# The first layer's input turned by TensorE's transposes and ScalarE's copies, in place of VectorE's block transposition of a second load, for 17 of 64 batches

## The chip, the cores and the metric

The kernel runs on one core of a Trainium2 chip. The metric is the device time of one execution in microseconds (us), as the median of several runs.

## What is computed

The input x is 64 batches of 256 rows of 256 numbers (float32); a mask adj of 256 x 256 is common to all batches. Two layers follow each other, and each adds to x the result of a graph attention and then that of a feed-forward part:

```
x = x + gat0(layernorm(x), adj, W, a)      # 4 heads of 64, leaky slope 0.2, softmax over the mask, elu
x = x + layernorm(x) @ weight.T + bias
x = x + gat1(layernorm(x), adj, W, a)      # one head of 256, slope 0.01, relu
x = x + moe(layernorm(x))                  # 8 experts, the top 2 of each row by a router, gelu between two matmuls
```

The change concerns the very first matmul of a batch, h @ W of the first attention. TensorE contracts over partitions, so it needs x with the features on the partitions, that is, x transposed.

## The kernel before, in words

**Tiling.** A batch is held as 2 tiles of 128 rows (`NT` = 2), and its 256 features as 2 halves of 128 (`KT` = 2). The normalisation isn't applied to x: its mean is taken out of the weights (`center`), and its scale `rstd` is multiplied in behind the matmul.

**The order of the work.** The program is laid out by hand as one sequence of steps, three for each batch (`TICKS`). Each batch is a generator (`batch_layers`), and each yield hands over a rank: a positive rank ends the batch's part in this step and gives its place in the next, smaller ranks first; a negative rank only moves the rest back within the same step. A batch is in flight for some twenty steps, so that six or seven batches overlap. Work of other kinds is begun beside them: the preparation of weights (`setup`, with the packing of the experts' weights, L280 to L296) over the first batches; the routing of each chunk of 4 batches (`route`, L1067); and from the second chunk on two expert pairs per batch (`expert_pair`, L870: rows gathered by an expert, its two matmuls `hidden` and `product`, and a scatter to the output by GpSimd). Each engine then works through its own instructions strictly in that order.

**A batch, by its lines.** In its first step x0 (`xin`, loaded three batches ahead, L96) is read by VectorE for the statistics of the norm (L379, L380). Two steps later the input is turned (L606), and one step after that it is projected (`projected`, L470), on TensorE; ScalarE takes exponentials (L478) and VectorE scales (L486). The scores' terms go to DRAM and come back spread over all partitions (L616, L551); up to batch 17 ScalarE's queue issues these two DMAs, later SP's (`terms_queue`, L545, with `SETTLED` = 18). VectorE forms the scores z (L567), TensorE multiplies them with q (`attended`, L581), VectorE divides and adds (L588, L634, L643 to L646). x1 is transposed by TensorE (`transposed`, L454, copied by ScalarE, L460), multiplied with the feed-forward weights (pf, L655), and becomes x2 (L662). x2 is transposed in the same way; then follow layer 1's projection (L505), scores (L524, L529), attention (pv with tiles of 128 x 257, L581 again), `rel` (L683), x2 again (L689), the normalised rows xng (L712) and base (L718), their transposition and the router's product pl (L743), copied to lg by VectorE (L747).

**How the input is turned before.** For the first layer a second load (`load_blocks`, L101 to L110) brings x into `xblk`: four DMAs of 64 KB for each batch, in pieces of 64 numbers (256 bytes), so arranged that a transposition within blocks of 32 x 32 gives the wanted layout. They are issued by SP two batches ahead (`BLOCKS_AHEAD` = 2), at the place where a batch is turned. One VectorE instruction (`turned`, L115, L117) then writes `xT`. The three other transpositions of a batch (x1, x2, xng) are made by `transposed`: four TensorE transposes against `ident` into one bank of PSUM, and one copy by ScalarE. Given `blocks=True`, as for xng, it takes every second column of x for each half, the order of features which the weights of the first layer have too (`rows` in `gnn_weights`).

**Buffers.** The tiles `xT` come from a ring of four, the PSUM banks from a ring of eight that all matmuls and transposes share (`bank`, L79).

Of the kernel before, what the change touches and what calls it, by code (L numbers as in the profile page):

```python
# [9 lines left out]
F32 = mybir.dt.float32  # L10
# [5 lines left out]
P = 128  # L16
# [11 lines left out]
def kernel(  # L28
# [18 lines left out]
    B, N, D = x.shape  # L47
# [3 lines left out]
    KT = D // P  # L51
# [22 lines left out]
    work = ctx.enter_context(tc.tile_pool(name="work", bufs=2))  # L74
# [4 lines left out]
    def bank(name, shape):  # L79
        t = psum.tile([P, 2 * D], F32, tag="bank", name=name, bufs=8)  # L80
        n = 1
        for s in shape:
            n *= s
        t = t[:, :n]
        if len(shape) == 2:
            t = t.rearrange("p (a b) -> p a b", a=shape[0])
        elif len(shape) == 3:
            t = t.rearrange("p (a b c) -> p a b c", a=shape[0], b=shape[1])
        return t
# [11 lines left out]
    def load_blocks(b):  # L101


        t = io.tile([P, N // S, KT * S], F32, tag="xblk", name=f"xblk_{b}", bufs=3)
        for g in range(P // S):
            nc.sync.dma_start(
                out=t[g * S : (g + 1) * S],
                in_=x[b].rearrange("(c q) (g f) -> g q c f", q=S, g=P // S)[g],
            )
        return t  # L110
# [4 lines left out]
    def turned(dst, blocks):  # L115

        nc.vector.transpose(  # L117
            dst.rearrange("p k (c q) -> p k c q", q=S),
            blocks.rearrange("p c (a k) -> p k c a", k=KT),
        )  # L120
        return dst

    def by_block(ap):

        return ap.rearrange("p (a k) -> p k a", k=KT)

    AHEAD, BLOCKS_AHEAD = 3, 2
    PAIRED = CHUNKS[0] + CHUNKS[1] + 3
    SETTLED = CHUNKS[0] + CHUNKS[1] + CHUNKS[2] + CHUNKS[3] + 2
# [99 lines left out]
    xblk = {0: load_blocks(0)}  # L229
# [220 lines left out]
    def transposed(src, pool=work, tag="xT", bufs=4, blocks=False):  # L450
        pt = bank("pt", [KT, N])
        for t in range(NT):
            for k in range(KT):
                nc.tensor.transpose(  # L454
                    pt[:, k, t * P : (t + 1) * P],
                    by_block(src[:, t, :])[:, k] if blocks else src[:, t, k * P : (k + 1) * P],
                    ident,
                )
        dst = pool.tile([P, KT, N], F32, tag=tag, name="xT", bufs=bufs)
        nc.scalar.copy(dst, pt)  # L460
        return dst
# [72 lines left out]
    def send_terms(q, b):  # L534
# [7 lines left out]
        ud = ud.rearrange("c r -> (c r)").rearrange("(c p) -> c p", p=P)  # L542
        return ut, ud

    def terms_queue(b):  # L545

        return nc.scalar if b < SETTLED else nc.sync

    def spread_terms(b, ud, z):

        terms_queue(b).dma_start(  # L551
            out=z[:, NT - 1].rearrange("p t h i -> p (t h i)"),
            in_=rows_to_all(ud, S * S),
        )
# [36 lines left out]
    def batch_layers(b, c0, xng, lg):  # L591

        def first_norm():
            x0 = xin.pop(b)
            if b + AHEAD < B:
                xin[b + AHEAD] = load_batch(b + AHEAD)
            return x0, norm_stats(x0)[1]

        if b:
            x0, rstd = first_norm()  # L600
            yield 99
            yield 4
        xb = xblk.pop(b)
        if b + BLOCKS_AHEAD < B:
            xblk[b + BLOCKS_AHEAD] = load_blocks(b + BLOCKS_AHEAD)
        xT = turned(work.tile([P, KT, N], F32, tag="xT", name="xT", bufs=4), xb)  # L606
        if not b:
            x0, rstd = first_norm()
        yield 22
# [3 lines left out]
        if b:  # L613
            ut, ud = send_terms(q, b)
            yield -31
            terms_queue(b).dma_start(  # L616
                out=ud.rearrange("c (g r) -> g c r", g=G),
                in_=ut[2 : P : S // (NT * H), :],
            )
            yield -52  # L620
# [29 lines left out]
        xT = transposed(x1)  # L650
# [20 lines left out]
        xT = transposed(x2)  # L671
# [66 lines left out]
        xT = transposed(xe[:, :, :D], *dense_home(b), blocks=True)  # L738
# [15 lines left out]
    def dense_home(b):  # L754

        if b < ROUTED:
            return ()
        return (io, "xblk", 3) if b < ROUTED + 3 else (io, "xin", 6)
# [444 lines left out]
    def jobs():  # L1203
        b = done = taken = 0
        for c, nb in enumerate(CHUNKS + (1,) * DENSE):
            nt = nb * NT
            lg = keep.tile([P, nt, E], F32, tag="lg", name=f"lg_{c}", bufs=7)
            xng = []
            row0 = b * N
            done += nt  # L1210
            n = max(done - (E - 1) - taken, 0) if b < ROUTED else 0
            taken += n
            for i in range(nb):
                def job(b=b, c=c, i=i, nb=nb, nt=nt, n=n, lg=lg, xng=xng, row0=row0):
                    yield from batch_layers(b, i * NT, xng, lg)
                    if i == nb - 1:
                        if b >= ROUTED:
                            yield 65
                            yield from route_dense(b, lg)
                        else:  # L1220
                            yield from route(c, row0, nt, n, b == ROUTED - 1, xng, lg)
                yield job()
                b += 1
# [85 lines left out]
```

## Time and profile before

Three runs: 1524.20, 1528.13 and 1528.14 us, median 1528.13.

| Profiled execution | |
|---|---|
| its own time | 1528.82 us |
| span, first to last instruction | 1527.0 us |
| TensorE matmul / weight load, busy | 1431.3 us (94%) / 1266.2 us (83%) |
| VectorE | 1255.8 us (82%) |
| ScalarE | 1007.2 us (66%) |
| GpSimd | 871.9 us (57%) |
| mean granted TensorE clock | 0.974 of full speed |
| moved by DMA | 240.84 MB in 372852 packets, 264773 of them under 512 bytes |

Engines are PE (TensorE; PEld for its weight loads), DVE (VectorE), ACT (ScalarE), POOL (GpSimd) and SP (which issues DMAs); an engine's name with a q behind it is its queue of instructions. A line such as L117 is a line of the kernel before. In the lists of groups, "out<-in" gives the tiles written and read, x and a number how often. A list of waits gives the waiting engine, tile and line, then what it waited for, then the total in us, how often, and the longest. In a timeline the first two numbers are the start and the length in us, and a bracket at the end is the time the engine sat idle before, and what ended it.

### The profile page before, as it was taken

To read this page: it belongs to the slowest core of one execution; us is meant where nothing else is said; L and a number is where in the kernel's file an instruction comes from. 1 tells how busy PE (TensorE), PEld (TensorE's weight loads), DVE (VectorE), ACT (ScalarE), POOL (GpSimd) and SP (SyncE) were. 2 spreads that over 40 slices of the span, in tenths; PEclk is the share of its full clock that TensorE was granted. 3 is DMA by queue.
4 is the path that set the end of the run, shared out by engine and by line. 5 is a ranking of instruction groups with operands and counts; after the bars stand their busy time and mean duration, and the time that the engine had idled before them with its cause. 6 is when DMAs were issued, how large, how long until landed. Compare 5 with 4: busy or idle time off the path is not lost.

```text
span 1527.0 us, 29964 instructions
## 1 busy us (share of the span) xinstructions
PE 1431.3 (94%) x8066; PEld 1266.2 (83%) x8066; DVE 1255.8 (82%) x4436; ACT 1007.2 (66%) x2379; POOL 871.9 (57%) x845
## 2 busy tenths in 40 slices
PE   6899989899999999999999999998899989799992
PEld 5788778789898989999998989897788877678882
DVE  7889998889988888888889989899888878655541
ACT  1466666577777777777877777776678779643330
POOL 2212536355857676767667675756747676544444
PEclk9999999899999999999999999999999999989997
DMA  5752434567877878787778787877768676788743
GB/s 146 206 170 87 137 115 123 143 161 154 190 172 176 180 174 177 170 180 165 178 176 185 170 180 159 194 157 164 172 156 186 127 164 131 169 198 166 140 62 52
DMA packets 372852, 240.84 MB, mean 158 GB/s; under 512 B 264773, under 2 KB 334925, under 8 KB 372685
## 3 DMA queue, kind: packets, MB, share of 16 engines
q1 hardware_dynamic: 319768, 162.62, 43.4%
q0 software_dynamic: 48864, 66.33, 23.7%
q10 hardware_dynamic: 4052, 9.98, 2.0%
q8 instruction: 67, 1.10, 0.3%
q14 instruction: 101, 0.82, 0.2%
HBM read 150.46 MB, written 88.35 MB: 156 GB/s over the span
## 4 chain that ended last, share of the span: by engine, by line
PE 66%; DVE 18%; DMA 4%; issue 4%; ACT 4%; SPq 2%; POOL 1%; DVEq 0%; another core or an unknown queue 0%; POOLq 0%; ACTq 0%; PEldq 0%
PE pv L581 15%; PE ph L944 14%; PE py L959 14%; PE pf L655 5%; PE pq L470 5%; PE pq L505 5%; DVE z L567 4%; PE pt L454 4%; PE pl L743 2%; DMA xblk<-in_x_dram 1%; DMA out_dram<-y,xt 1%; DVE stats L379 1%; DVE x L644 1%; DVE x1b L646 1%; DVE x L662 1%
## 5 line engine op out<-in xcount | busy, mean ns | idle before, releaser
L980 POOL DMA_INDIRECT out_dram<-y,xt x258 | 413.5, 1603 | 198.2 <-issue 63.8
L581 PE MATMUL pv<-q,z 128*128 128x65 f32 (+1 forms) x2560 | 370.4, 301 | 0.3
L581 PEld LDWEIGHTS pv<-q,z 128*128 128x128 f32 x2560 | 336.6, 196 | 13.3 <-DVE z L567 0.8
L1050 POOL DMA_INDIRECT xs<-xng,pos x244 | 263.4, 1079 | 65.4 <-issue 60.0
L959 PE MATMUL py<-w2s,hT 128*128 (+1 forms) x1224 | 280.7, 380 | 5.6 <-ACT hT L950 5.5
L959 PEld LDWEIGHTS py<-w2s,hT 128*128 128x128 f32 x1224 | 229.1, 191 | 37.4 <-ACT hT L950 8.0
L944 PE MATMUL ph<-sT,we 128*128 128x256 f32 x1032 | 244.4, 387 | 12.9 <-DMA we<-wpack 6.5
L567 DVE SCALAR_TENSOR_TENSOR z<-z,q,mask 128x256 f32<-128x256 f32 x504 | 231.5, 482 | 11.8 <-DMA z<-terms 2.8
L944 PEld LDWEIGHTS ph<-sT,we 128*128 128x128 f32 x1032 | 198.7, 195 | 42.2 <-issue 7.2
L937 ACT ACTIVATE y<-y,w 128x256 f32<-128x256 f32 x258 | 113.0, 498 | 114.3 <-DVE y L969 111.5
L460 ACT COPY xT<-pt 128x512 f32<-128x512 f32 x192 | 112.8, 587 | 105.1 <-PE pt L454 77.3
L950 ACT ACTIVATE hT<-ph,we 128x256 f32<-128x256 f32 x306 | 123.7, 472 | 63.5 <-PE ph L944 39.3
L407 POOL TENSOR_SCALAR rstd<-mv 128x4 f32<-128x4 f32 (+1 forms) x66 | 15.6, 236 | 255.2 <-DVE mv L380 201.6
L425 ACT ACTIVATE off<-x,sums 128x256 f32<-128x256 f32 x256 | 129.4, 505 | 10.4 <-DVE x L662 2.6
L505 PE MATMUL pq<-wx,xT 128*128 128x259 f32 x512 | 127.1, 391 | 7.3 <-ACT xT L460 4.1
L969 DVE TENSOR_TENSOR y<-py,b2s 128x512 f32<-128x512 f32 x129 | 85.7, 685 | 57.9 <-PE py L959 41.6
L470 PE MATMUL pq<-wx,xT 128*128 128x268 f32 x512 | 128.2, 394 | 2.4 <-DVE xT L117 1.8
L655 PE MATMUL pf<-wfT,xT 128*128 128x256 f32 x512 | 125.7, 390 | 0.0
L683 ACT ACTIVATE rel<-pv,rinv 128x256 f32<-128x256 f32 x128 | 53.7, 468 | 99.6 <-DVE rinv L588 66.6
L505 PEld LDWEIGHTS pq<-wx,xT 128*128 128x128 f32 x512 | 95.3, 192 | 28.2 <-ACT xT L460 8.2
L470 PEld LDWEIGHTS pq<-wx,xT 128*128 128x128 f32 x512 | 98.0, 192 | 21.5 <-DVE wx L168 1.3
L655 PEld LDWEIGHTS pf<-wfT,xT 128*128 128x128 f32 x512 | 95.9, 197 | 11.1 <-issue 0.2
(172 smaller groups left out, 2378.0 us busy)
## 6 DMA issues: line engine op xcount, KB each, us to landing
we<-wpack SPq DMA_DIRECT2D x145, 288.0 KB
xr<-xs SPq DMA_DIRECT2D x516, 64.0 KB
z<-terms SPq DMA_DIRECT2D x46, 512.0 KB
xblk<-in_x_dram SPq DMA_DIRECT2D x256, 64.0 KB
xin<-in_x_dram SPq DMA_DIRECT2D x64, 256.0 KB
out_dram<-base SPq DMA_DIRECT2D x61, 256.0 KB
z<-terms ACTq DMA_DIRECT2D x17, 512.0 KB
out_dram<-y,xt POOLq DMA_INDIRECT x258
```

The costliest lines, as they stand in the source:

```text
L425: nc.scalar.activation(off, src[:, t, :], AF.Square, bias=sums[:, t : t + 1], scale=-float(D), accum_out=sq[:, at + t : at + t + 1],)
L470: nc.tensor.matmul(pq.rearrange("p h c -> p (h c)"), xT[:, k, t * P : (t + 1) * P], wx[:, k, :], start=(k == 0), stop=(k == KT - 1),)
L505: nc.tensor.matmul(pq, xT[:, k, t * P : (t + 1) * P], wx1[:, k, :], start=(k == 0), stop=(k == KT - 1),)
L567: nc.vector.scalar_tensor_tensor(z[:, j, :, h, :], terms, q[:, j, h, HD + 2 : HD + 3], masks[0][:, j, :].rearrange("p (t i) -> p t i", t=N ...
L581: nc.tensor.matmul(pv[:, h, :], z(j, h, t), q[:, j, h, : d + 1], start=(j == 0), stop=(j == NT - 1),)
L655: nc.tensor.matmul(pf[:, t, :], xT[:, k, t * P : (t + 1) * P], wfT[:, k, :], start=(k == 0), stop=(k == KT - 1),)
L937: nc.scalar.activation(y[:, t, :], y[:, t, :], AF.Copy, scale=w[:, t : t + 1])
L944: nc.tensor.matmul(ph[:, f, :], we[:, k * D + f * P : k * D + (f + 1) * P], xT[:, k, :], start=(k == 0), stop=(k == KT - 1),)
L950: nc.scalar.activation(hT[:, f, :], ph[:, f, :], AF.Gelu, bias=we[:, C_B1 + f : C_B1 + f + 1])
L959: nc.tensor.matmul(py[:, t, :], hT[:, f, t * P : (t + 1) * P], w2s[:, e, f * D : (f + 1) * D].rearrange("p e c -> p (e c)"), start=(f == 0 ...
L980: d = nc.gpsimd.indirect_dma_start(out=out_rows, out_offset=bass.IndirectOffsetOnAxis(ap=xt[:, t, 0:1].bitcast(I32), axis=0), in_=y[:, t, ...
L1050: d = nc.gpsimd.indirect_dma_start(out=xs_d[: E * CAP * PAIR, :], out_offset=bass.IndirectOffsetOnAxis(ap=at, axis=0), in_=xe, in_offset=None,
```

## The change

For batches 2 to 18 (`by_tensor`) the second load and the VectorE transposition fall away. In their place `transposed` takes x0, the tile that is loaded for the statistics anyway: four TensorE transposes into a bank and one ScalarE copy. In the step in which the input is turned, the rank goes from 4 to 38, behind the transposes of x2 (rank 36) and ahead of layer 1's attention (rank 40) of other batches. Batches 0 and 1 and those from 19 on are as before; the blocks of batch 19 are loaded in batch 17.

```diff
+    def by_tensor(b):
+
+        return BLOCKS_AHEAD <= b <= SETTLED
+
...
         if b:
             x0, rstd = first_norm()
             yield 99
-            yield 4
-        xb = xblk.pop(b)
-        if b + BLOCKS_AHEAD < B:
+            yield 38 if by_tensor(b) else 4
+        if b + BLOCKS_AHEAD < B and not by_tensor(b + BLOCKS_AHEAD):
             xblk[b + BLOCKS_AHEAD] = load_blocks(b + BLOCKS_AHEAD)
-        xT = turned(work.tile([P, KT, N], F32, tag="xT", name="xT", bufs=4), xb)
+        if by_tensor(b):
+            xT = transposed(x0, blocks=True)
+        else:
+            xT = turned(work.tile([P, KT, N], F32, tag="xT", name="xT", bufs=4), xblk.pop(b))
         if not b:
             x0, rstd = first_norm()
```

## Prediction

> **What bounds the kernel now.** I began with the page's totals: TensorE is busy for 94% of the span, VectorE for 82%. That is a mean over stages, and the change touches batches 2 to 18 only. So I took the starts of the block transpositions of L117 as marks: batch 2 at 27.60 us, 6 at 84.33, 9 at 126.92, 19 at 287.72, 21 at 327.54. Busy times between such marks:
>
> ```profile
> 84.33:126.92 42.59, 42.30 (x268) 38.45 (x268) 38.11 (x129) 31.12 (x84) 9.14 (x15) 0.96 0.46 139
> 126.92:287.72 160.80, 149.37 (x902) 129.85 (x901) 149.63 (x549) 101.88 (x276) 67.35 (x86) 0.97 0.40 118
> 220.11:237.82 17.71, 16.07 (x81) 13.94 (x79) 14.83 (x56) 9.19 (x27) 8.57 (x10) 0.81 0.54 153
> 327.54:427.99 100.45, 100.45 (x597) 90.54 (x596) 90.52 (x311) 76.76 (x182) 68.33 (x65) 1.00 0.80 175
> ```
> After the stretch and its length come PE, PE's weight loads, VectorE, ScalarE and GpSimd, then TensorE's granted clock. From 327 us on TensorE is never idle. From 84 to 127 it is nearly so, and a batch there takes 13.22 us. Between 127 and 288 us, ten batches of 16.1 us, both are at 93%, and the waits decide. All of VectorE's waits in that stretch, and the largest of TensorE's between 130 and 300 us:
>
> ```profile
> DVE x L662 <- issue: 2.2, 1, 2.2
> DVE q L486 <- ACT q L478: 0.9, 1, 0.9
> DVE y L969 <- DVE mv L380: 0.6, 1, 0.6
> ```
> ```profile
> PE pd L524 <- ACT ex L512: 6.3, 12, 2.0
> PE pt L454 <- DVE x L662: 4.8, 7, 1.1
> ```
> VectorE waits 3.7 us in 160.8. The rest that isn't busy lies between instructions that follow each other without a wait. TensorE waits every batch, for what hangs on VectorE. So **VectorE sets the pace from 127 to 288 us**, TensorE from 84 to 127 and after about 300. The chain of waits agrees: between 150 and 250 us it is led by VectorE lines, from 309 us on it holds TensorE alone.
>
> Last, the operations concerned:
>
> ```profile
> L117 DVE STREAM_TRANSPOSE xT<-xblk x64: 651/703/727, 9.9 to 1203.5; 128x512 f32<-128x512 f32 x64
> L454 PE MATMUL pt<-ident,xng x256: 272/283/417, 80.1 to 1330.7; 128*128 128x128 f32 x128
> L460 ACT COPY xT<-pt x31: 562/567/620, 128.3 to 286.8; 128x512 f32<-128x512 f32 x31
> ```
>
> **What the skill says.** "Vector Engine: DVE Perf Modes", The three transpose paths: VectorE turns 32x32 blocks only, into SBUF; TensorE turns a full 128x128, into PSUM. Hence the blocked second load before, and a copy after. "TensorE: Matmul & The Clock Gate", Part 4: about 275 ns for a transpose in a kernel; it doesn't count as busy for the clock. The trace has 273 ns (x) and 283 ns (xng), but pipelined. The same page, Part 1: after an idle window of about 3.4 us the clock is halved. The trace agrees: 0.81 granted over 220 to 238 us, with matmuls at half speed. "DMA: Bandwidth & Descriptors", Issuing engines are not separate DMA queues: all DMAs share the same 16 engines. This case shows contention at 68 us, below.
>
> **The change, part by part.** In the built program's order VectorE loses 17 block transpositions. TensorE gains 17 times four transposes, between those of x2 and the matmuls pv of layer 1. ScalarE gains 17 copies, each right behind the copy of x2. SP loses 68 loads.
>
> (1) *VectorE, batches 9 to 18.* At 220.11 a transposition starts, and the next instruction (L643) at 220.74: the place is worth 0.63 us, less than the 0.70 of its duration. Ten batches paced by VectorE: **-6.3 us**. Late next is TensorE: its 13.22 a batch becomes 13.72, under the 15.3 that VectorE then needs (16.1 less 0.63 and its share of waits). The loop through both holds too: from L662 to the reciprocal of layer 1 VectorE has 4.6 us of work, then 4.0; TensorE's way over x2's transposes, the new ones and pv takes 2.7, then 3.2.
>
> (2) *TensorE, batches 6 to 8.* Four blocked transposes of xng hold the engine from 110.36 to 110.87, 0.50 us; four of x take 0.44. x0 is read in blocks, as xng is: 0.50. Alone, with latency, it would be 0.68; 0.44 to 0.68 bounds it. Three batches: **+1.5 us**. In batches 9 to 18 it lies inside TensorE's waits; without this cover it would cost 5 us.
>
> (3) *ScalarE.* 17 copies of 0.57 us. Behind the copy are `rel` (L683) and the exponentials of layer 1. `rel` waits for the reciprocal, 28.9 us in 9 batches of the stretch: covered. In batches 7 and 8 it waits 1.5 us after a copy (101.95 to 103.48): covered. Uncovered: up to 0.57 each. Zero.
>
> (4) *Batches 2 to 5.* The transpositions at 27.60 and 56.84 are on the chain, with 0.62 and 0.57: **-1.2 us**. Batch 3's isn't; its z waits for a DMA: 0. At batch 5 VectorE waits for the spread terms, which left together with four block loads:
>
> ```profile
> 68.30 1.81 SPq L106 DMA_DIRECT2D xblk<-in_x_dram  x4
> 68.36 0.34 ACTq L551 DMA_DIRECT2D z<-terms  x1
> ...
> 74.24 3.75 DVE L567 SCALAR_TENSOR_TENSOR z<-z,q,mask 128x256 f32<-128x256 f32 x8 [1.64 <-DMA z<-terms]
> ```
> Here 5.86 us from issue to use; at 41.61, with no block loads beside it, 4.76. I take **-1.1 us**. Ends: 0 (the weight loads fill the room) and -1.6, the whole idle time. The 68 issues of 0.45 us that SP is rid of only bring the loads behind them forward. They are 4.5 of 240.8 MB.
>
> (5) *New waits.* The transposes wait for x0, which VectorE's statistics read two steps earlier, and for a bank. One more bank per batch moves the ring of eight on: the second half of the projection (L470) now waits for the copy of lg (L747), where before the transposes of x1 did (0.7 us in two cases). Behind it queue x1's transposes, pd and pv. At 207.9 TensorE would come to it, 208.4 with (2); lg was copied at 208.63, and is now 0.63 earlier, 208.0: no wait. Bounds 0 to 0.4 for each of ten batches; 0.
>
> (6) *Clock.* Cold stretches follow gaps without matmuls:
>
> ```profile
> 223.95 0.60 PE L454 MATMUL pt<-ident,x 128*128 128x128 f32 x4
> 225.99 0.32 PE L524 MATMUL pd<-ident,ex 128*128 128x128 f32 x1 [1.44 <-ACT ex L512]
> 226.51 0.32 PE L524 MATMUL pd<-ident,ex 128*128 128x128 f32 x1 [0.20 <-ACT ex L512]
> 226.67 4.90 PE L581 MATMUL pv<-q,z 128*128 128x65 f32 x32
> ```
> From 223.95 to 226.67 there are only transposes and waits. Then pv takes 4.90 instead of 3.68, and VectorE's 2.2 us for pf at 236 is the price. VectorE 0.63 earlier and TensorE 0.5 later shorten the gap by 1.1. I count half the price: **-1.1 us**. Ends: -2.2, and -4.2 more if the stretch near 295 us goes too (pv 6.72 for 3.52, pf 2.68 for 1.73); above, new cold stretches elsewhere, +2.2 each.
>
> Sum: -6.3 + 1.5 - 1.2 - 1.1 - 1.1 = -8.2 us. The profiled execution took 1528.82 us, 1527.0 of span and 1.8 around it; it lies 0.7 over the median, with two of three runs. 1528.8 - 8.2 = 1520.6; against the median 1519.9. **I say 1520.5.** After batch 19 TensorE's order is unchanged and TensorE never waits in the stretch read, so what was won should reach the end.
>
> **The rivals.**
> *A. More: the cold stretches go too.* For it: gaps shrink. Against: the one near 295 us belongs to batch 19, whose transposition stays on VectorE. -8.2 - 1.1 - 4.2: 1515. Chance 0.17.
> *B. Little: the wait moves.* The new transposes lengthen VectorE's loop over TensorE by 0.50 and leave 0.13 of 0.63, 1.3 us in ten batches; contention stays. -1.3 + 1.5 - 1.2: 1527.8. For it: TensorE is at 93% there too. Against: VectorE's 3.7 us of waits. Chance 0.20.
> *C. Slower: the clock.* The new transposes stand in the gap between pl and pv (217.3 to 218.53, then 1.8 us). If they count as idle there, each cold stretch costs 2.2. Without the clock term the sum is -7.1, so it is slower from the fourth; with six 1528.8 - 7.1 + 13.2 = 1535. Against: 1.8 us is less than the 2.7 that went cold. Chance 0.08.
> The forecast, 1517 to 1523.5, has 0.55.
>
> **How the numbers follow.** About 0.3%, 4.6 us, is what a measurement can tell from no change: the line is 1523.5. Faster: forecast and A, 0.72; same: B, 0.20; slower: C, 0.08. The range goes from 1513 (A with the full contention term) to 1527, short of B's centre; about 0.2 is left out.
>
> **What would show it.** Right: the ten batches after 127 us take about 15.4 us each, VectorE still with few waits; batches 7 and 8 take 13.7; `rel` still waits for the reciprocal; z's wait at batch 5 is gone. Wrong: waits of VectorE for pf or a reciprocal of tenths in every batch (B), a clock under 0.95 between 127 and 288 us (C), or the time given back after 300 us.

## The result, and the profile after

| | before | after |
|---|---|---|
| median of 7 runs each | 1524.20 us (1517.64 to 1532.57) | 1516.68 us (1509.31 to 1523.71) |
| ratio after / before | | 0.994, 95% interval 0.991 to 0.9969 |
| profiled execution: span | 1527.0 us | 1514.9 us |
| granted TensorE clock, mean | 0.974 | 0.985 |

The change makes the kernel faster by 7.5 us in the medians, by 5 to 14 us within the interval. (The ratio isn't that of the medians, which is 0.995.) The forecast was 8.2 us less, and 1520.5 us: the difference came out, but the time lies 3.8 us lower, just under the 1517 to 1523.5 of the forecast's middle and near rival A's 1515, since the seven runs of the kernel before have a median of 1524.20 us where the first three had 1528.13. Single executions of one kernel lie up to 15 us apart here, up to 23 in the longest series below, so the stages are compared and not the spans. The profile after is a favourable one: its granted clock, 0.985, is the highest of the seven runs (0.970 to 0.985).

Since VectorE's transposition is gone for 17 batches, the marks are now the starts of a batch's first projection matmul (L470 in both kernels). The same stretches, batches 6 to 8 and 9 to 18, by busy time of each engine, granted clock and DMA; first before, then after, where batch 15 and the batches 21 to 25 follow:

```profile
91.16:130.83 39.67, 39.67 (x260) 36.05 (x259) 37.45 (x126) 28.78 (x79) 10.01 (x15) 1.00 0.45 131
130.83:289.24 158.41, 146.98 (x890) 127.84 (x888) 147.31 (x541) 99.12 (x267) 66.61 (x85) 0.97 0.39 115
```
```profile
91.44:132.53 41.09, 41.09 (x272) 37.48 (x271) 36.48 (x124) 31.53 (x82) 9.83 (x15) 1.00 0.25 78
132.53:282.95 150.42, 144.00 (x925) 128.52 (x924) 141.31 (x530) 103.64 (x275) 70.16 (x85) 1.00 0.35 108
220.69:238.31 17.62, 15.89 (x99) 13.91 (x98) 16.78 (x64) 13.02 (x33) 10.62 (x12) 1.00 0.38 131
323.54:424.43 100.89, 100.87 (x600) 90.84 (x598) 91.31 (x313) 77.41 (x183) 69.06 (x65) 1.00 0.80 173
```
Batches 6 to 8, TensorE's, take 41.09 us instead of 39.67: 13.70 each for 13.22. The ten batches from 9 to 18 take 150.42 instead of 158.41, and the granted clock there is 1.00 instead of 0.97. From batch 21 on five batches take 20.2 us each, 20.1 before.

VectorE's waits between 126 and 283 us, over the relieved batches, and two of TensorE's there (line numbers are 4 higher than before from L545 on, 6 from L606 on):

```profile
DVE q L486 <- ACT q L478: 0.9, 1, 0.9
DVE x L668 <- PE pf L661: 0.9, 2, 0.6
DVE y L975 <- PE pv L585: 0.6, 1, 0.6
DVE rinv L592 <- PE pv L585: 0.5, 1, 0.5
```
```profile
PE pt L454 <- DVE x L668: 3.3, 7, 0.7
PE pd L524 <- ACT ex L512: 0.7, 2, 0.5
```
VectorE still hardly waits: 2.9 us in 157. TensorE's wait for the exponentials at pd was this in the same batches before, from 130.83 to 289.24 us:

```profile
PE pd L524 <- ACT ex L512: 4.3, 11, 1.4
```
It has fallen from 4.3 us to 0.7. So VectorE still paces this stage, with less to do. The new transposes stand on TensorE like this (start, length):

```profile
86.79 0.84 PE L454 MATMUL pt<-ident,x 128*128 128x128 f32 x4
87.47 0.64 PE L454 MATMUL pt<-ident,xin 128*128 128x128 f32 x4
87.94 1.90 PE L585 MATMUL pv<-q,z 128*128 128x257 f32 x8
```
Listed with 0.64, they hold the engine from 87.47 to 87.94, 0.47 us.

What did not go as forecast is the beginning. From batch 2 to batch 6 the profile after takes 63.23 us, before 62.71. VectorE's waits for the spread terms, of which one should have gone, grew from 2.8 us to 5.7 between 28 and 92 us. First before, then after:

```profile
DVE z L567 <- DMA z<-terms: 2.8, 2, 1.6
```
```profile
DVE z L571 <- DMA z<-terms: 5.7, 2, 3.4
DVE x L650 <- ACT e L646: 2.7, 2, 1.5
```
The wait of 1.64 us that the prediction had named is gone (z starts at 76.28 us without it). But of the two before it the first grew from 1.19 us to 2.32, and the second, none before, is 3.42. And ScalarE's queue, which issues these DMAs, was itself held up. Its timeline, and its one long wait between 48 and 60 us:

```profile
51.06 0.52 ACTq L622 DMA_DIRECT2D terms<-ut  x1
55.68 0.33 ACTq L555 DMA_DIRECT2D z<-terms  x1
```
```profile
ACT e L646 <- DMA wpack<-wt: 8.1, 1, 8.1
```
Between sending the terms and fetching them lie 4.6 us; before, at the same batch, 1.7 (52.27 to 53.94). By the profile the last thing that ScalarE waited for was a store of packed expert weights (wpack). That is an inference from semaphores, and one case speaks against the store alone: in e1_loads, below, such a store leaves SP at 50.81 us, 0.3 us after the terms, and the fetch follows these after 1.7 us.

### The profile page after: what moved, and what is told of

Read it like the earlier page. It is cut to its first block, busy times and chain, and to the rows that moved or that the text cites. A ratio compares the mean times of both kernels' runs of the same rounds, so it can differ in the third digit from the quotient of the medians.

```text
span 1514.9 us, 29999 instructions
## 1 busy us (share of the span) xinstructions
PE 1421.4 (94%) x8134; PEld 1261.2 (83%) x8134; DVE 1245.9 (82%) x4419; ACT 1017.4 (67%) x2396; POOL 875.8 (58%) x845
## 5 line engine op out<-in xcount | busy, mean ns | idle before, releaser
L585 PE MATMUL pv<-q,z 128*128 128x65 f32 (+1 forms) x2560 | 362.6, 296 | 0.4
L585 PEld LDWEIGHTS pv<-q,z 128*128 128x128 f32 x2560 | 329.9, 193 | 13.0 <-DVE z L571 1.1
L460 ACT COPY xT<-pt 128x512 f32<-128x512 f32 x209 | 121.3, 588 | 99.2 <-PE pt L454 76.6
L470 PE MATMUL pq<-wx,xT 128*128 128x268 f32 x512 | 128.1, 394 | 1.5 <-ACT xT L460 0.7
L470 PEld LDWEIGHTS pq<-wx,xT 128*128 128x128 f32 x512 | 97.8, 192 | 20.7 <-DVE wx L168 1.3
```

The source lines that it names most:

```text
L470: nc.tensor.matmul(pq.rearrange("p h c -> p (h c)"), xT[:, k, t * P : (t + 1) * P], wx[:, k, :], start=(k == 0), stop=(k == KT - 1),)
L585: nc.tensor.matmul(pv[:, h, :], z(j, h, t), q[:, j, h, : d + 1], start=(j == 0), stop=(j == NT - 1),)
```

## The experiments

The theory after the result: VectorE's relief gives 8 us in batches 9 to 18; TensorE's added work costs 1.4 in batches 6 to 8; and in batches 3 to 6 a gain is lost because SP, rid of the block loads, issues the experts' weights earlier and so onto the terms. Rivals: that the fuller TensorE keeps its clock up, and this is the gain; that the gain is the DMAs' relief; that the loss at the beginning comes from where the transposes stand. All stage times are from one profile each (us, between the starts of batches named). The ratios are from the timed runs, each to runs of the kernel before beside them; the changed kernel was timed only in the first series:

| kernel | 2 to 9 | 9 to 19 | 19 to 20 | ratio to before, 95% interval |
|---|---|---|---|---|
| before | 102.38 | 158.41 | 23.68 | 1 |
| after | 104.32 | 150.42 | 20.38 | 0.994 (0.991 to 0.9969) |
| e1_both | 102.57 | 158.05 | 20.40 | 0.9978 (0.9959 to 0.9997) |
| e1_loads | 98.45 | 151.52 | 23.92 | 0.9906 (0.987 to 0.9942) |
| e1_late | 100.88 | 150.41 | 22.62 | 0.9928 (0.9892 to 0.9964) |
| e1_early | 103.85 | 158.61 | 22.61 | 0.9989 (0.9967 to 1.001) |
| e2_spaced | 96.86 | 151.92 | 23.90 | 0.9897 (0.9861 to 0.9932) |
| e2_before_spaced | 97.46 | 163.14 | 23.66 | 0.9968 (0.9945 to 0.9991) |
| e2_best | 95.63 | 150.46 | 23.89 | 0.9871 (0.9832 to 0.9911) |
| e2_all | 106.15 | 150.80 | 19.38 | 1.0052 (1.003 to 1.0075) |

**e1_both: the new work is added, the old stays.** Against the changed kernel:

```diff
-            yield 38 if by_tensor(b) else 4
-        if b + BLOCKS_AHEAD < B and not by_tensor(b + BLOCKS_AHEAD):
+            yield 4
+        if b + BLOCKS_AHEAD < B:
             xblk[b + BLOCKS_AHEAD] = load_blocks(b + BLOCKS_AHEAD)
+        xT = turned(work.tile([P, KT, N], F32, tag="xT", name="xT", bufs=4), xblk.pop(b))
         if by_tensor(b):
-            xT = transposed(x0, blocks=True)
-        else:
-            xT = turned(work.tile([P, KT, N], F32, tag="xT", name="xT", bufs=4), xblk.pop(b))
+            yield -38
+            transposed(x0, tag="xTspare", bufs=1, blocks=True)
```
To make room it also has 8 buffers for y instead of 9.

> The transposes and copies are added for batches 2 to 18, with the result unused (into a tile of its own; one buffer fewer for the experts' y), while VectorE's transposition and the second load stay. Marks are the starts of the first projection matmul (L470) of a batch: before, batch 9 at 130.8 us, batches 9 to 19 in 158.4, 19 to 20 in 23.7; after, 132.5, 150.4 and 20.4. If VectorE sets the pace: batch 9 some 1.4 us later than before (three batches of 13.7), 9 to 19 in 158 +-1, so about 1.5 us slower than before. If TensorE's added work lengthens VectorE's loop: 9 to 19 in 160 to 163, 3 to 6 us slower. If the added work on TensorE is what keeps the clock up: no stretch at half clock between 127 and 310 us, 19 to 20 in about 20.4, and 2 to 4 us faster than before.

Batches 9 to 19 take 158.05 us: ten times four transposes and a copy cost nothing there, and gain nothing. So it is VectorE's relief that makes 150.4 of it, and neither TensorE's load nor the loop through both engines. Batches 6 to 8 take 41.44. The kernel came out about 3 us faster than before, not 1.5 slower, and the interval (0.9959 to 0.9997) just leaves 1 out. That is what the clock rival had expected, and one more of its signs is there: batch 19 to 20 took 20.40 us without a stretch at half clock. But its gain would have to lie in batches 9 to 18, and there the time is as before and so is the cold stretch (half clock) near 230 us. So that rival is refuted for these batches; what makes the whole 3 us faster isn't shown. The place near 230 us:

```profile
222.77 0.60 PE L454 MATMUL pt<-ident,x 128*128 128x128 f32 x4
224.45 0.32 PE L524 MATMUL pd<-ident,ex 128*128 128x128 f32 x1 [1.08 <-ACT ex L512]
...
225.13 5.46 PE L585 MATMUL pv<-q,z 128*128 128x65 f32 x32
```
With VectorE relieved, the same place in the profile after (what stands for "..." is a second pd in both):

```profile
222.49 0.60 PE L454 MATMUL pt<-ident,x 128*128 128x128 f32 x4
223.59 0.32 PE L524 MATMUL pd<-ident,ex 128*128 128x128 f32 x1 [0.50 <-ACT ex L512]
...
224.28 3.68 PE L585 MATMUL pv<-q,z 128*128 128x65 f32 x32
```
The stretch with only transposes and waits lasts 2.7 us before, 2.4 with the work added, 1.8 after, and only in the last does pv run at full speed all through. In all ten profiles batch 15 to 16 takes 17.6 us where VectorE is relieved there, and 20.1 to 21.8 where it isn't.

**e1_loads: the block loads stay, with their data unused for batches 2 to 18.**

```diff
-            yield 38 if by_tensor(b) else 4
-        if b + BLOCKS_AHEAD < B and not by_tensor(b + BLOCKS_AHEAD):
+            yield 4
+        if b + BLOCKS_AHEAD < B:
             xblk[b + BLOCKS_AHEAD] = load_blocks(b + BLOCKS_AHEAD)
+        blocks = xblk.pop(b)
         if by_tensor(b):
+            yield -38
             xT = transposed(x0, blocks=True)
         else:
-            xT = turned(work.tile([P, KT, N], F32, tag="xT", name="xT", bufs=4), xblk.pop(b))
+            xT = turned(work.tile([P, KT, N], F32, tag="xT", name="xT", bufs=4), blocks)
```

> The changed kernel, but the second load is still issued for every batch, its data unused for 2 to 18. If VectorE's relief is the gain: batches 9 to 19 in about 150.4 us as in the changed kernel. If the relief of the DMAs is: about 158. If SP, freed from these loads, brings the experts' weights forward onto the terms of batches 3 to 5, then here batch 6 comes at 88.5 to 90 us (91.2 before, 91.4 after), batch 9 at 130 to 131, and the whole is 1 to 2.5 us faster than the changed kernel; if the loss there has another cause, batch 6 stays at 91.4 or comes later.

Batch 6 comes at 85.7 us, earlier still than expected, and batches 2 to 9 take 98.45 us instead of 104.32. Loading 4.5 MB that nobody reads makes the changed kernel 5.9 us quicker there. For the whole kernel the ratio is lower too, but its interval overlaps that of the changed kernel. VectorE's wait for the terms between 28 and 92 us falls back:

```profile
DVE z L571 <- DMA z<-terms: 2.3, 2, 1.9
```
The last load of an expert's w1 starts at 75.4 us here, at 78.3 before and at 68.6 in the changed kernel. In batches 9 to 19 these loads cost 1.1 us, and a cold stretch near 170 us (batch 11 to 12 in 16.79 for 15.12) more than accounts for it. So the DMAs' relief isn't the gain.

**e1_late and e1_early: half of the change each.**

```diff
-        return BLOCKS_AHEAD <= b <= SETTLED
+        return 9 <= b <= SETTLED            # e1_late
+        return BLOCKS_AHEAD <= b <= 8       # e1_early
```

> Only batches 9 to 18 are turned by TensorE. If the gain is VectorE's from 127 us on: batch 9 at 130.8 as before, 9 to 19 in 150 to 151.5, about 9 us faster than before and 1.5 faster than the changed kernel. If the gain needs the earlier batches (fewer loads, an earlier packing): less than 6 us faster than before.

> Only batches 2 to 8 are turned by TensorE. By the stages: batch 9 at 132.5 us as in the changed kernel, then 9 to 19 in about 158.4 and 19 to 20 in 20.4 to 23.7 as before: 1 to 2 us slower than before. If the early batches carry part of the gain: at least 2 us faster than before.

Both came out as the stages say: the late half has the whole gain (150.41; about 10 us in the medians, 1512.07 for 1521.62), and the early half none (158.61; 1522.63 for 1521.62). Batches 2 to 6 take 63.23 us in the early half as in the changed kernel. In the late half, whose order there is the kernel before's, they take 59.92, 2.8 us less than in the profile before: so much can single profiles of the same order differ in this stretch. Of it 2.2 us lie in batch 5 to 6, with a clock of 0.90 before and 1.00 in the late half.

**e2_spaced and e2_before_spaced: the experts' weights packed one per batch.**

```diff
-            if step >= SETUP_AT and setup:
+            if step >= SETUP_AT and setup and (len(setup) > E + 1 or phase == 1):
```

> The changed kernel, but the experts' weights are packed one expert per batch instead of one per step, so that their loads are spread over batches 2 to 11. If the loss in batches 3 to 6 comes from these loads meeting the terms: from batch 2 to 9 some 98.5 us, as with the second load kept (98.45; 104.3 in the changed kernel, 102.4 before), and about 5 us faster than the changed kernel, 11 to 13 faster than before. If it comes from the way the transposes stand on TensorE or ScalarE: 103 to 105 us, no faster than the changed kernel.

> The kernel before with the same spacing of the packing. If the packing hurts only where SP is freed to run it early: 2 to 9 in 100 to 102.5 us and less than 3 us faster than before. If the packing itself holds both kernels up: 97 to 99 us, 4 to 6 us faster.

Spread out, the packing lets the changed kernel take 96.86 us from batch 2 to 9, 7.5 less, and VectorE waits nowhere for the terms between 20 and 130 us. The whole took 1507.27 us for 1520.48. That the loads of the experts' weights are what delays the terms is shown here a second time, without the unused loads. The kernel before gains in that stretch too, 4.9 us (3.4 against e1_late, whose order is the same up to batch 6): the packing held up both, and the change made it worse by the difference, 2.5 to 4.0 us. Its whole gain was smaller, 3 us in the medians, and its profile shows two cold stretches in batches 9 to 19 (163.14 us), one of them near 230 us and 10 us long.

**e2_best: spaced, and batches 6 to 8 left to VectorE.**

```diff
-        return BLOCKS_AHEAD <= b <= SETTLED
+        return BLOCKS_AHEAD <= b <= 5 or 9 <= b <= SETTLED
```

> As the spaced one, but batches 6 to 8, which TensorE paces, are turned by VectorE: 0.47 us less in each of three, so 2 to 9 in about 97 us, 9 to 19 in 150.4, and 12 to 14 us faster than before. If those batches are not TensorE's to pace once the packing is spread: no faster than the spaced one.

Batches 6 to 8 take 40.15 us instead of 41.09, 2 to 9 in all 95.63. With 1504.55 us for 1520.48 it has the lowest median of all: 16 us under the kernel before, where the changed kernel is 7.5 under it. From e2_spaced it isn't told apart by the timed runs: the two intervals overlap.

**e2_all: every batch from 2 on.**

```diff
-        return BLOCKS_AHEAD <= b <= SETTLED
+        return BLOCKS_AHEAD <= b
```

> All batches from 2 on are turned by TensorE. If TensorE sets the pace after batch 20: a batch there takes 20.55 to 20.6 us instead of 20.1, so over some 36 batches 17 us more, and with the last ones 17 to 22 us slower than the changed kernel, about 10 to 14 slower than before. If the transposes hide beside other work there: within 4 us of the changed kernel.

From batch 20 to batch 55 the time goes from 703.0 to 717.3 us, and against the other kernels of these runs (700.6 to 700.8) by 0.47 us a batch. The kernel is slower than before by 4.6 to 11.4 us, a little less than expected. After batch 20 the same edit that gains 0.6 us a batch costs half a microsecond.

## Why the prediction was right, and where it wasn't

(1) *VectorE, -6.3 us: right.* Of the 8.0 us between batches 9 and 19, 2.55 fall to batch 15, and the nine others give 5.45, 0.61 each; the forecast had 0.63. (The 15.3 us that it says VectorE then needs for a batch is 15.1 with the 3.7 us of waits that it names; nothing rests on it. Measured were 15.04, the clock's part included.)

(2) *TensorE, +1.5 us: right.* 1.42 measured, and 1.42 again between the two spaced kernels; 0.47 a batch for 0.50.

(3) *ScalarE, nothing; (5) the wait for lg, nothing: right.* With both added in e1_both, batches 9 to 19 take what they took. No wait of the second projection for lg shows in the lists of waits after.

(4) *Batches 2 to 5, -2.3 us: wrong.* In the two profiles it is +0.5, and against e1_late, with the order of before in these batches, +3.3. The step that failed is "The 68 issues of 0.45 us that SP is rid of only bring the loads behind them forward", counted at nothing. Those loads are the experts' weights, and forward is where the terms of batches 3 to 6 travel. With the block loads kept, in e1_loads, the stretch takes 57.33 us instead of 63.23, 5.9 less. Of these, 3.4 are VectorE's shorter waits for the terms (2.3 us for 5.7), and part of the rest is the clock behind such a wait: batch 4 to 5 takes 17.55 us at 0.90 in the changed kernel and 13.46 at 1.00 in e1_loads. The gain that the step claimed was there: with the packing spread out, the stretch takes 55.77 us with the change and 57.79 without, 2.0 less where the forecast had 2.3. Against that gain the +0.5 and +3.3 mean a cost of 2.5 to 5.3 us. So removing a contender for the DMAs removed the delay that kept a larger contender away. Whether the terms lost more to shared DMA engines or to their own issue, held until a store of weights had landed, was not separated.

(6) *Clock, -1.1 us: right for batch 15, but too small.* Batch 15 lost its cold stretch in every kernel with VectorE relieved: 2.55 less 0.61, so 1.9 us, nearly the whole price of 2.2. The stretch near 295 us, rival A's, vanished in the profile after (19 to 20 in 20.38 for 23.68). But it stayed in e1_loads, e1_late, e2_spaced and e2_best, whose batches 9 to 18 are the same, and vanished in e1_both, where VectorE isn't relieved. It isn't the change's doing; what decides it stays open. The step took the length of a gap for what decides, and so did its case against rival C, that 1.8 us is less than the 2.7 that went cold. That is wrong already in the profile before: at 157 us half clock followed a gap of 1.6 us (the last section has the lines).

Of the Trainium skill, "TensorE: Matmul & The Clock Gate", Part 4, that transposes don't count as busy for the clock, fits the cold pv behind 2.4 to 2.7 us of transposes and waits; no run tests it alone. The prediction says that the trace agrees with Part 1 of that page, half clock after an idle window of about 3.4 us. Only the halving agrees: gaps that went cold here are as short as 1.6 us, and the measurement decides. The page that the prediction calls "Vector Engine: DVE Perf Modes" is titled "VectorE: DVE Perf Modes".

Of the rivals, A's event, no half clock near 295 us, did occur in the profile after, by luck. B is refuted by VectorE's few waits and by e1_both. C, slower by cold stretches behind the new transposes, is refuted for the whole by the ratio, and the clock is 1.00 over batches 9 to 18 after. But its event occurred: e1_loads and e2_spaced have a cold stretch right behind new transposes, between the starts of batches 11 and 12, and take 151.52 and 151.92 us for the ten batches; e1_late, e2_best and e2_all have none, and take 150.41 to 150.80. The sum was right also because misses cancel: +2.8 in step (4) against -0.8 in (6) and the luck of batch 19, which is 3.3 of the 9.6 us that the two profiles differ by up to batch 20. After batch 20 the ten profiles differ by up to 20 us, or 9 without e2_all, in no order of what was changed, which is why only the timed ratio speaks of the whole.

## What to carry to other kernels

Move work off an engine only in the stage that this engine paces: the same edit gained 0.6 us a batch where VectorE set the pace, and cost 0.47 where TensorE did. When a DMA is removed from an in-order queue, ask what stands behind it and what that will meet when it comes earlier; spreading the bulk loads out was worth about 6 us more here, by medians whose ratios have overlapping intervals. Show a cost by adding the new work while keeping the old, and by keeping a removed transfer with its data unused: the difference is then one cause and not two.

## What the runs showed that was not expected

A kernel that loads 4.5 MB more than the changed one, in pieces of 256 bytes, and doesn't use them, was no slower: 1509.95 us against 1521.62 before, ratio 0.9906, where the changed kernel has 0.994. That it is the faster of the two is shown for batches 2 to 9 (98.45 us for 104.32), and only likely for the whole, where the intervals overlap.

And the length of a gap, a stretch of TensorE with only transposes and waits, doesn't tell whether half clock follows. Before, a gap of 1.6 us, from the end of pl to pv, with pv at half clock behind it (0.50 from 157.20 to 160.61 us):

```profile
154.65 1.06 PE L743 MATMUL pl<-rT,xT 128*128 128x8 f32 x8 [0.56 <-ACT xT L460]
...
157.34 3.52 PE L581 MATMUL pv<-q,z 128*128 128x257 f32 x8
```
A gap of the same kind between the starts of batches 11 and 12, the new transposes included, is 1.88 us long both in e1_loads and in e1_late. In the first pv is slow, at a clock of 0.50 from 168.07 us on, in the second not:

```profile
164.81 1.06 PE L751 MATMUL pl<-rT,xT 128*128 128x8 f32 x8 [0.30 <-ACT xT L460]
...
167.75 3.32 PE L585 MATMUL pv<-q,z 128*128 128x257 f32 x8
```
```profile
167.45 1.06 PE L749 MATMUL pl<-rT,xT 128*128 128x8 f32 x8 [0.30 <-ACT xT L460]
...
170.39 1.90 PE L585 MATMUL pv<-q,z 128*128 128x257 f32 x8
```
And after, at batch 19, pv runs at full speed behind 3.2 us:

```profile
284.76 0.60 PE L454 MATMUL pt<-ident,x 128*128 128x128 f32 x4
...
287.98 3.68 PE L585 MATMUL pv<-q,z 128*128 128x65 f32 x32
```
In all ten profiles the stretches at half clock between 30 and 340 us last 3.41, 6.83 or 10.24 us, and they start whole multiples of 3.41 us apart. So the clock changes on a grid of 3.41 us. How a gap falls on that grid may be what decides; no run tests this. A cold stretch that comes or goes in one profile therefore says little about a change; batch 15, alike in ten profiles, says more.
